# Cross-attention: the values' third round on halves of the array's rows, in two banks; inputs normed a step ahead of their transposes

## The chip, the cores and the metric

The kernel runs on one NeuronCore of a Trainium2 chip. Its engines are TensorE (PE, with the weight loads shown apart as PEld), VectorE (DVE), ScalarE (ACT), GpSimd (POOL) and SyncE (SP); here POOL and SP also issue the DMAs. The metric is the device time of one launch in microseconds (us).

## The reference

The input x is 128 sequences of 32 tokens with 512 channels, the context 128 x 257 x 512. All data is float32. Three blocks follow each other, each on a layer norm of x and added to x: cross-attention, a gated delta-rule layer, and a feed-forward with quantised weights. Only the first is changed:

```python
def _layernorm(x, axis=-1, eps=1e-05):
    m = jnp.mean(x, axis=axis, keepdims=True)
    v = jnp.var(x, axis=axis, keepdims=True)
    return (x - m) / jnp.sqrt(v + eps)
...
q = jnp.einsum('bsd,ed->bse', x, wq)
k_new = jnp.einsum('bsd,ed->bse', x, wk)
v_new = jnp.einsum('bsd,ed->bse', x, wv)
k = jnp.concatenate([k_cache, k_new], axis=1)
v = jnp.concatenate([v_cache, v_new], axis=1)
scores = jnp.einsum('bqd,bkd->bqk', q, k) * scale
attn = jax.nn.softmax(scores, axis=-1)
out = jnp.einsum('bqk,bkd->bqd', attn, v)
return jnp.einsum('bqd,ed->bqe', out, wo)
...
x = x + _L0_xattn_ref(_layernorm(x, axis=-1), mask, ctx_2048, ctx_2048, wq, wk, wv, wo)
```

The context is both the cache of keys and that of values. Each token attends to the 257 rows of its sequence's context and to the 32 tokens of its own sequence: 289 keys.

## The kernel before

Cross-attention takes 128 tokens (four sequences, a "tile") at a time, in 32 steps. Four tiles make a group of 512 tokens; there are eight groups.

At the head of a group, queries and keys of its 512 tokens are projected: 32 float32 matmuls of 128x128x512 (L395), their results copied by ACT and DVE in turn. `hT` holds the normed inputs with channels on partitions; it has been made during the group before.

Each of a group's four steps then does this, and the parts belong to three tiles, so that PE has work while the other engines are busy with the softmax:

- `new_rows` (n): the values of the new tokens are projected (L293), copied to `vn` (DVE, L298), and stored by four POOL DMAs (L300) into `vx`, a tile of 33 partitions: the context's last row (an SP DMA, L289) and 32 new rows, for each of four sequences. A POOL copy (L301) puts the new keys behind the 257 loaded ones in `kall`.
- `turned` (n-1): the 128x289 weights `pr` are transposed on PE in three pieces of 128, 128 and 33 columns (L330) and copied to `prT` by ACT (L332, the first two) and DVE (L333, the third).
- `project` (n-2): the output projection (L360), the residual sum (DVE, L364), a POOL store, and the new statistics (`mean_var`, L81 and L82).
- `values` (n-1): for each sequence j a matmul with 32 columns of weights, so that four run on four column strips of the array. Rounds 0 and 1 take the context's rows, two to a partition (`cx`), 512 columns each; round 2 takes the 33 rows of `vx`. All accumulate in one PSUM bank `av`, which DVE scales into `ao` (L348).
- `weights` (n): the scores (L313), their maximum (L318, L319), the exponential on ACT (L322), the reciprocal of its sum (L323).
- `flipped` (n-1): `ao` is transposed (L97) and copied by ACT (L353).

Two generators are advanced within a step. `quantised_weights` reads the feed-forward's weights in pieces (`raw`), first for a sum of magnitudes (L197), then for three DVE operations (L212 to L214) and a POOL store. `prepared` makes the next group's `hT` in seven slots of which each step takes two, one ahead of the scores and one at its end: loads of three inputs; nothing; load of the fourth; statistics of three; statistics of the fourth and `inverse` (a root on ACT, L246, and a reciprocal on DVE, L247); two inputs normed (`xn`, L241), transposed (L97) and copied by ACT (L242); the other two.

Each engine works through its own queue in order. The order in a queue is not quite that of the source: a scheduler lays it out when the program is built. Root and exponential need different tables in ACT, loaded by an instruction of their own. All PSUM tiles of the stage come from one pool of eight banks; tiles named `xn` have two buffers, `raw` three.

`InOrder` (already there, used in later stages) wraps an engine so that each of its instructions is ordered behind the one before; its instructions are recorded at line 151.

Of the kernel before, what the change touches and what calls it, by code (L numbers as in the profile page):

```python
# [10 lines left out]
FP = mybir.dt.float32  # L11
BF = mybir.dt.bfloat16
AF = mybir.ActivationFunctionType
ALU = mybir.AluOpType
# [4 lines left out]
P = 128  # L19
D = 512  # L20
DC = D // P
NB = 128
T = 32
NT = NB * T
LC = 257
NK = LC + T
# [3 lines left out]
SG = 512  # L30
# [27 lines left out]
class Ctx:  # L58
# [16 lines left out]
        self.eps2 = const.tile([P, 1], FP, name="eps2")  # L75
        nc.vector.memset(self.eps2, LN_EPS * RMS_EPS)

    def mean_var(self, pool, x, mv):

        st = pool.tile([P, 6], FP, name="bn_st")  # L80
        self.nc.vector.bn_stats(st, x)  # L81
        self.nc.vector.bn_aggr(mv, st)  # L82

    def factors(self, mv, rs):

# [133 lines left out]
def cross_attention(g: Ctx, x, ctx_kv, ctxT, wqT, wkT, wvT, woT, x1, stats, scales, ffn_weights):  # L219
# [5 lines left out]
    tc, nc = g.tc, g.nc  # L225
# [3 lines left out]
        ("a_wk", 2), ("a_st", 4), ("a_ps", 8, PSUM),  # L229
    )  # L230
    with stack:
        def load_x(s, i):
            t = xp.tile([P, D], FP, name="xt")
            r = s * SG + i * P
            nc.sync.dma_start(t, x[r : r + P, :])
            return t

        def normed(hT, i, xt, mv, rstd):

            xn = wk.tile([P, D], FP, name="xn")  # L240
            nc.vector.tensor_scalar(xn, xt, mv, rstd, ALU.subtract, ALU.mult)  # L241
            nc.scalar.copy(hT[:, :, i * P : (i + 1) * P], g.transposed(ps, xn, g.ident))  # L242

        def inverse(mv, n):
            rstd = st.tile([P, n], FP, name="rstd")
            nc.scalar.activation(rstd, mv[:, :, 1], AF.Sqrt, bias=g.ln_eps)  # L246
            nc.vector.reciprocal(rstd, rstd)  # L247
            return rstd

        def prepared(s, xt, hT):  # L250


            n = SG // P
            xt.extend(load_x(s, i) for i in range(n - 1))
            yield
            yield
            xt.append(load_x(s, n - 1))
            yield
            mv = st.tile([P, n, 2], FP, name="mv")
            for i in range(n - 1):  # L260
                g.mean_var(st, xt[i], mv[:, i, :])
            yield
            g.mean_var(st, xt[n - 1], mv[:, n - 1, :])
            rstd = inverse(mv, n)
            yield
            for half in range(2):
                for i in range(half * n // 2, (half + 1) * n // 2):
                    normed(hT, i, xt[i], mv[:, i, 0:1], rstd[:, i : i + 1])
                yield

        def load_keys(gi):

# [12 lines left out]

        def new_rows(gi, kall, hT, kT, i):

            vx = cp.tile([T + 1, 4, D], FP, name="vx")
            nc.sync.dma_start(vx[0:1], ctx_kv[gi * 4 : gi * 4 + 4, LC - 1, :].unsqueeze(0))  # L289

            pv = ps.tile([P, D], FP, name="ps")
            for dc in range(DC):
                nc.tensor.matmul(  # L293
                    pv, hT[:, dc, i * P : (i + 1) * P], w["v"][:, dc, :],
                    start=dc == 0, stop=dc == DC - 1,
                )
            vn = wk.tile([P, D], FP, name="vn")
            nc.vector.tensor_copy(vn, pv)  # L298
            for j in range(4):
                nc.gpsimd.dma_start(vx[1 : T + 1, j, :], vn[j * T : (j + 1) * T, :])  # L300
            nc.gpsimd.tensor_copy(  # L301
                kall[:, :, :, LC:NK],
                kT[:, :, i * P : (i + 1) * P].rearrange("p c (b t) -> p c b t", b=4),
            )
            return vx
# [18 lines left out]
            return pr, rs  # L324

        def turned(pr):
            pp = ps.tile([P, 3, P], FP, name="ps")
            for r in range(3):
                m = P if r < 2 else T + 1
                nc.tensor.transpose(pp[0:m, r, :], pr[:, r * P : r * P + m], g.ident)  # L330
            prT = wk.tile([P, 3, P], FP, name="prT")
            nc.scalar.copy(prT[:, 0:2, :], pp[:, 0:2, :])  # L332
            nc.vector.tensor_copy(prT[0 : T + 1, 2, :], pp[0 : T + 1, 2, :])  # L333
            return prT

        def values(cx, vx, prT, rinv):

            av = ps.tile([P, D], FP, name="ps")
            for r in range(3):
                for j in range(4):  # L340
                    js = slice(j * T, (j + 1) * T)
                    if r < 2:
                        lhsT, rhs = prT[:, r, js], cx[:, j, r, :]
                    else:
                        lhsT, rhs = prT[0 : T + 1, 2, js], vx[:, j, :]
                    nc.tensor.matmul(av[js, :], lhsT, rhs, start=r == 0, stop=r == 2)
            ao = wk.tile([P, D], FP, name="ao")
            nc.vector.tensor_scalar_mul(ao, av, rinv)  # L348
            return ao

        def flipped(ao):
# [4 lines left out]
        def project(n, xt, aoT):  # L356

            po = ps.tile([P, D], FP, name="ps")
            for dc in range(DC):
                nc.tensor.matmul(  # L360
                    po, aoT[:, dc, :], w["o"][:, dc, :], start=dc == 0, stop=dc == DC - 1
                )
            xo = wk.tile([P, D], FP, name="xo")
            nc.vector.tensor_add(xo, po, xt)  # L364
            nc.gpsimd.dma_start(x1[n * P : (n + 1) * P, :], xo)
            g.mean_var(st, xo, stats[0][:, n, :])

        xt = [load_x(0, i) for i in range(SG // P)]
        kalls, cxs, quantised = {}, {}, None
# [9 lines left out]
        cxs[1] = load_values(1)  # L379

        hT = sp.tile([P, DC, SG], FP, name="hT")
        for i in range(SG // P):
            mv = st.tile([P, 1, 2], FP, name="mv0")
            g.mean_var(st, xt[i], mv[:, 0, :])
            normed(hT, i, xt[i], mv[:, 0, 0:1], inverse(mv, 1))
        for s in range(NT // SG):
            if s == NT // SG - 1:
                g.factors(*(t[:, 0:EARLY] for t in stats))
# [2 lines left out]
            for wn, dst in ((w["q"], qT), (w["k"], kT)):  # L391
                for ec in range(DC):
                    pp = ps.tile([P, SG], FP, name="ps")
                    for dc in range(DC):
                        nc.tensor.matmul(  # L395
                            pp, wn[:, dc, ec * P : (ec + 1) * P], hT[:, dc, :],
                            start=dc == 0, stop=dc == DC - 1,
# [9 lines left out]
            for i in range(SG // P):  # L407
                n = s * (SG // P) + i
                kall = kalls.pop(n)
                vx = new_rows(n, kall, hT, kT, i)  # L410
                if soft is not None:
                    m, xm, vm, pr, rs = soft
# [468 lines left out]
def delta_out_mlp(  # L881
# [14 lines left out]
    with stack:  # L896
# [105 lines left out]
        def mlp(b):  # L1002
# [14 lines left out]
            for i in range(NTL):  # L1017
                pd = psm.tile([P, D], FP, name="pm")
                for fc in range(FC):
                    nc.tensor.matmul(  # L1020
                        pd, mT[:, fc, i * P : (i + 1) * P], wd[:, fc, :],
                        start=fc == 0, stop=fc == FC - 1,
                    )
                xo = zp.tile([P, D], FP, name="xo", bufs=2)
                mark[:] = [nc.vector.tensor_add(xo, pd, xs[i]).ins]
                n = b * NTL + i
                nc.gpsimd.dma_start(x2[n * P : (n + 1) * P, :], xo)
                g.mean_var(st, xo, mv2[:, n, :])
                z = zp.tile([P, D], FP, name="z")
                nc.vector.tensor_scalar(z, xo, mv2[:, n, 0:1], None, ALU.subtract)  # L1030
                z = butterflies(nc, z, zp.tile([P, D], FP, name="zb"))
                nc.gpsimd.dma_start(z2[n * P : (n + 1) * P, :], z)
                yield 9.5
# [534 lines left out]
```

## Time and profile before

| what | value |
|---|---|
| median of 3 runs | 2940.22 us (2938.33 to 2943.78) |
| the profiled execution | 2938.77 us, span 2937.0 us |
| cross-attention | 0 to some 690 us of the span |
| PE busy over the span | 2823.2 us (96%) |
| DVE, ACT, POOL busy | 1995.4, 1033.0, 682.5 us |
| granted TensorE clock, mean | 0.988 |

The span runs from the first to the last instruction of one execution recorded by the hardware profiler. A row of the order of time gives start, duration, engine, line, operation, out<-in, the tile of the array that a matmul uses (rows*columns), operand shapes and the count of instructions merged; the brackets give the engine's idle time ahead of it and what ended it. A float32 matmul appears as two instructions, a transpose as one. Of matmuls in a row the ends overlap the next starts, so the distance of starts is the time that one takes of PE. Line 151 stands for everything issued through `InOrder` and similar wrappers.

### The profile page before, as it was taken

The page shows a single profiled execution, that of the slowest core. Times are in us where ns is not written, and L with a number is a line of the kernel's source. Part 1 is how long each engine was busy: PE and PEld are TensorE (multiplying, and loading weights), DVE is VectorE, ACT ScalarE, POOL GpSimd, SP SyncE. Part 2 cuts the span into 40 slices and gives each one's busy share as a digit, 9 for nine tenths or more (in the row PEclk, how much of TensorE's full clock was granted, in tenths as well). Part 3 has the DMA queues.
Part 4 walks back from the last instruction along what each step waited for, and adds up shares of the span by engine and source line. Part 5 has one row for each costly group of instructions (what it writes and reads, how often), then busy time and mean ns, then how long its engine had stood idle before and what let it go on. Part 6 is the DMA issues. An engine that isn't in the chain of part 4 may idle for free.

```text
span 2937.0 us, 42773 instructions
## 1 busy us (share of the span) xinstructions
PE 2823.2 (96%) x15895; PEld 1658.6 (56%) x15958; DVE 1995.4 (68%) x3317; ACT 1033.0 (35%) x1766; POOL 682.5 (23%) x974
## 2 busy tenths in 40 slices
PE   8999999997999899999999999999999989999997
PEld 3434343443443344566676767777777756666664
DVE  3353544325599995678787878888722289999996
ACT  1111111213666466521122212112211146776774
POOL 1121212212777677321212111101000000000000
PEclk9999999999999999999999999999999999999999
DMA  9898998874555545841414141313231124434433
GB/s 316 275 306 295 337 315 278 280 243 123 149 165 155 163 141 145 242 140 56 130 54 132 56 130 52 122 57 98 71 108 33 35 74 90 87 81 88 89 71 69
DMA packets 342815, 429.64 MB, mean 146 GB/s; under 512 B 149712, under 2 KB 250192, under 8 KB 340176
## 3 DMA queue, kind: packets, MB, share of 16 engines
q1 hardware_dynamic: 305696, 324.36, 37.0%
q0 software_dynamic: 36912, 102.55, 11.7%
q8 instruction: 127, 2.08, 0.3%
q14 instruction: 80, 0.66, 0.1%
HBM read 288.88 MB, written 94.37 MB: 130 GB/s over the span
## 4 chain that ended last, share of the span: by engine, by line
PE 59%; DVE 10%; issue 2%; DMA 2%; POOL 1%; ACT 1%; SPq 1%; ACTq 0%; DVEq 0%; POOLq 0%
PE ps L151 18%; PE pm L1009 9%; PE pm L1020 9%; PE pm L1012 9%; PE pp L151 5%; PE ps L983 4%; DVE W L503 2%; DVE pr L497 2%; DVE acc L625 2%; PE ps L953 2%; PE pg L151 1%; PE pn L151 1%; DMA xs<-x 1%; POOL kk L541 1%; DVE m L151 1%
## 5 line engine op out<-in xcount | busy, mean ns | idle before, releaser
L1009 PE MATMUL pm<-hT,wg 128*128 128x256 f32 x1408 | 343.1, 386 | 0.2 <-ACT hT L998 0.2
L1012 PE MATMUL pm<-hT,wu 128*128 128x256 f32 x1408 | 336.8, 382 | 1.3 <-DVE wu L1070 1.3
L497 DVE TENSOR_TENSOR pr<-L,W 128x1984 f32<-128x1984 f32 (+30 forms) x248 | 307.3, 1239 | 9.1 <-DMA L<-ld 4.6
L503 DVE TENSOR_TENSOR W<-W,pr 128x1984 f32<-128x1984 f32 (+30 forms) x248 | 309.7, 1249 | 2.8
L1020 PE MATMUL pm<-wd,mT 128*128 128x512 f32 x704 | 307.4, 592 | 0.0
L1009 PEld LDWEIGHTS pm<-hT,wg 128*128 128x128 f32 x1408 | 263.9, 191 | 51.0 <-issue 11.5
L1012 PEld LDWEIGHTS pm<-hT,wu 128*128 128x128 f32 x1408 | 268.7, 191 | 38.7 <-DVE wu L1070 1.6
L1020 PEld LDWEIGHTS pm<-wd,mT 128*128 128x128 f32 x704 | 132.4, 190 | 160.2 <-issue 160.2
L151 PE MATMUL ps<-wq,qT 128*128 128x512 bf16 x930 | 215.5, 379 | 6.2 <-ACT t L151 4.6
L1014 ACT ACTIVATE sg<-pm 128x256 f32<-128x256 f32 x176 | 67.4, 383 | 331.4 <-PE pm L1009 319.7
L1015 DVE TENSOR_TENSOR mT<-pm,sg 128x256 f32<-128x256 f32 x176 | 74.0, 420 | 158.7 <-PE pm L1012 155.0
L151 PEld LDWEIGHTS <-qT 128*128 128x128 bf16 x960 | 94.0, 98 | 105.3 <-issue 5.5
L151 DVE TENSOR_TENSOR mb<-m 128x1024 f32<-128x1024 f32 x128 | 153.2, 1217 | 0.1
L151 DVE TENSOR_TENSOR m<-mb 128x1024 f32<-128x1024 f32 x128 | 150.8, 1219 | 1.2
L1343 POOL DMA_DIRECT2D xo<-x x31 | 26.4, 851 | 526.4 <-ACT xo L151 492.0
L151 ACT ACTIVATE t<-ps,magic,qs 128x512 f32<-128x512 f32 x158 | 115.7, 781 | 39.5 <-DVE qs L151 39.4
L537 POOL DMA_DIRECT2D ld<-kk x128 | 93.6, 731 | 147.6 <-ACT kk L151 120.5
L541 POOL TENSOR_TENSOR kk<-kk,cm 128x256 f32<-128x256 f32 x128 | 126.3, 987 | 2.7
L151 PEld LDWEIGHTS ps<-hd,mT 128*128 128x128 f32 x1024 | 119.1, 192 | 8.9 <-ACT mT L151 4.8
L151 PE MATMUL ps<-hd,mT 128*128 128x128 f32 x1024 | 119.8, 275 | 4.0 <-ACT mT L151 4.0
L151 PE MATMUL ps<-wq,q2T 128*128 128x512 bf16 x481 | 116.2, 384 | 5.4 <-DMA q2T<-q 3.7
L151 PE MATMUL pp<-hT,wk 128*128 128x512 f32 x256 | 120.3, 614 | 0.7 <-ACT hT L151 0.7
(224 smaller groups left out, 4751.2 us busy)
## 6 DMA issues: line engine op xcount, KB each, us to landing
kall<-in_ctxT_dram SPq DMA_DIRECT2D x32, 2056.0 KB
cx<-in_ctx_dram SPq DMA_DIRECT2D x32, 2048.0 KB
x<-xo POOLq DMA_DIRECT2D x64, 256.0 KB, 3.5
ld<-kk POOLq DMA_DIRECT2D x128, 128.0 KB, 2.6
pd<-kk POOLq DMA_DIRECT2D x128, 128.0 KB, 2.6
L<-ld SPq DMA_DIRECT2D x32, 512.0 KB
pe<-pd SPq DMA_DIRECT2D x256, 64.0 KB
kqm<-kq SPq DMA_DIRECT2D x448, 32.0 KB
```

The lines of the kernel that those rows point to most:

```text
L151: got = method(*args, **kw)
L497: nc.vector.tensor_mul(pr[:, 0:n], bc(L[:, s, :, s + 1 : T].rearrange("p h t -> p t h"), HD), w[:, s].unsqueeze(1).to_broadcast([P, n, H4, ...
L503: nc.vector.tensor_sub(w[:, s + 1 :], w[:, s + 1 :], pr[:, 0:n])
L537: nc.gpsimd.dma_start(ld[r].rearrange("(i p) f -> p i f", p=P), kk[:, 0].rearrange("p i h t -> p i (h t)"))
L541: nc.gpsimd.tensor_mul(q, q, cm.unsqueeze(1).to_broadcast([P, 2 * H4, T]))
L625: last = nc.vector.scalar_tensor_tensor(acc[:, :, d:], pp[:, :, : T - d], cw[n][:, ec, TAPS - 1 - d : TAPS - d], acc[:, :, d:], ALU.mult, ...
L983: nc.tensor.matmul(pw, oT[:, i, dc, :], wo[:, dc, :], start=dc == 0, stop=dc == DC - 1)
L1009: nc.tensor.matmul(pg, wg[:, dc, fs], hT[:, dc, :], start=dc == 0, stop=dc == DC - 1)
L1012: nc.tensor.matmul(pu, wu[:, dc, fs], hT[:, dc, :], start=dc == 0, stop=dc == DC - 1)
L1014: nc.scalar.activation(sg, pg, AF.Silu)
L1015: mark[:] = [nc.vector.tensor_mul(mT[:, fc, :], pu, sg).ins]
L1020: nc.tensor.matmul(pd, mT[:, fc, i * P : (i + 1) * P], wd[:, fc, :], start=fc == 0, stop=fc == FC - 1,)
```

## The change

- `vx` gets 128 partitions and half the width: partitions 0 to 32 hold channels 0 to 255 of the 33 rows, partitions 64 to 96 channels 256 to 511. Its context row comes by two DMAs and the new rows by eight.
- `turned` puts the third piece of the transposed weights on both sets of partitions: the transpose as before, and a plain matmul of the same 33 columns with the identity, whose result goes to PSUM partitions 64 to 96. DVE copies both.
- `values` works in two PSUM banks, one for each half of the channels. Rounds 0 and 1 go by halves, 256 columns each; in round 2 each sequence has two matmuls, one on the upper and one on the lower half of the array's rows. DVE scales each bank by itself.
- `prepared` moves the statistics one slot ahead, and the normed inputs stand ahead of their transposes: two are normed in the fifth slot, the sixth transposes them and norms the other two, the seventh transposes those. `inverse` becomes `deviation`, without the reciprocal.
- The first group's inputs go through an `InOrder` DVE: one's statistics, then the reciprocal and norm of the one before.
- `mean_var` takes the engine as an argument. The calls outside this stage do the same as before.

```diff
         def prepared(s, xt, hT):
             n = SG // P
             xt.extend(load_x(s, i) for i in range(n - 1))
             yield
+            mv = st.tile([P, n, 2], FP, name="mv")
             yield
             xt.append(load_x(s, n - 1))
+            for i in range(n - 1):
+                g.mean_var(nc.vector, st, xt[i], mv[:, i, :])
             yield
-            mv = st.tile([P, n, 2], FP, name="mv")
-            for i in range(n - 1):
-                g.mean_var(st, xt[i], mv[:, i, :])
+            g.mean_var(nc.vector, st, xt[n - 1], mv[:, n - 1, :])
+            rstd = deviation(mv, n)
+            nc.vector.reciprocal(rstd, rstd)
             yield
-            g.mean_var(st, xt[n - 1], mv[:, n - 1, :])
-            rstd = inverse(mv, n)
-            yield
-            for half in range(2):
-                for i in range(half * n // 2, (half + 1) * n // 2):
-                    normed(hT, i, xt[i], mv[:, i, 0:1], rstd[:, i : i + 1])
-                yield
+            xn = []
+            for i in range(n + 2):
+                if 2 <= i:
+                    across(hT, i - 2, xn[i - 2])
+                if i < n:
+                    xn.append(normed(nc.vector, xt[i], mv[:, i, 0:1], rstd[:, i : i + 1]))
+                if i % 2:
+                    yield
...
-            vx = cp.tile([T + 1, 4, D], FP, name="vx")
-            nc.sync.dma_start(vx[0:1], ctx_kv[gi * 4 : gi * 4 + 4, LC - 1, :].unsqueeze(0))
+            vx = cp.tile([P, 4, D // 2], FP, name="vx")
+            for h in range(2):
+                nc.sync.dma_start(
+                    vx[h * P // 2 : h * P // 2 + 1],
+                    ctx_kv[gi * 4 : gi * 4 + 4, LC - 1, halves[h]].unsqueeze(0),
+                )
...
             for j in range(4):
-                nc.gpsimd.dma_start(vx[1 : T + 1, j, :], vn[j * T : (j + 1) * T, :])
+                for h in range(2):
+                    r = h * P // 2 + 1
+                    nc.gpsimd.dma_start(vx[r : r + T, j, :], vn[j * T : (j + 1) * T, halves[h]])
...
         def turned(pr):
             pp = ps.tile([P, 3, P], FP, name="ps")
-            for r in range(3):
-                m = P if r < 2 else T + 1
-                nc.tensor.transpose(pp[0:m, r, :], pr[:, r * P : r * P + m], g.ident)
+            for r in range(2):
+                nc.tensor.transpose(pp[:, r, :], pr[:, r * P : (r + 1) * P], g.ident)
             prT = wk.tile([P, 3, P], FP, name="prT")
+            nc.tensor.transpose(pp[last[0], 2, :], pr[:, 2 * P : NK], g.ident)
+            nc.tensor.matmul(pp[last[1], 2, :], pr[:, 2 * P : NK], g.ident, start=True, stop=True)
             nc.scalar.copy(prT[:, 0:2, :], pp[:, 0:2, :])
-            nc.vector.tensor_copy(prT[0 : T + 1, 2, :], pp[0 : T + 1, 2, :])
+            for rows in last:
+                nc.vector.tensor_copy(prT[rows, 2, :], pp[rows, 2, :])
             return prT

         def values(cx, vx, prT, rinv):
-            av = ps.tile([P, D], FP, name="ps")
-            for r in range(3):
-                for j in range(4):
-                    js = slice(j * T, (j + 1) * T)
-                    if r < 2:
-                        lhsT, rhs = prT[:, r, js], cx[:, j, r, :]
-                    else:
-                        lhsT, rhs = prT[0 : T + 1, 2, js], vx[:, j, :]
-                    nc.tensor.matmul(av[js, :], lhsT, rhs, start=r == 0, stop=r == 2)
+            av = [ps.tile([P, D // 2], FP, name="ps") for _ in range(2)]
+            for r in range(2):
+                for h in range(2):
+                    for j in range(4):
+                        js = slice(j * T, (j + 1) * T)
+                        nc.tensor.matmul(
+                            av[h][js, :], prT[:, r, js], cx[:, j, r, halves[h]],
+                            start=r == 0, stop=False,
+                        )
+            for j in range(4):
+                js = slice(j * T, (j + 1) * T)
+                for h in range(2):
+                    nc.tensor.matmul(
+                        av[h][js, :], prT[last[h], 2, js], vx[last[h], j, :], start=False, stop=True
+                    )
             ao = wk.tile([P, D], FP, name="ao")
-            nc.vector.tensor_scalar_mul(ao, av, rinv)
+            for h in range(2):
+                nc.vector.tensor_scalar_mul(ao[:, halves[h]], av[h], rinv)
             return ao
...
-        for i in range(SG // P):
-            mv = st.tile([P, 1, 2], FP, name="mv0")
-            g.mean_var(st, xt[i], mv[:, 0, :])
-            normed(hT, i, xt[i], mv[:, 0, 0:1], inverse(mv, 1))
+        dve = InOrder(tc, nc.vector)
+        got = []
+        for i in range(SG // P + 1):
+            if i < SG // P:
+                mv = st.tile([P, 1, 2], FP, name="mv0")
+                g.mean_var(dve, st, xt[i], mv[:, 0, :])
+                got.append((mv[:, 0, 0:1], deviation(mv, 1)))
+            if i:
+                mv, rstd = got[i - 1]
+                dve.reciprocal(rstd, rstd)
+                across(hT, i - 1, normed(dve, xt[i - 1], mv, rstd))
```

With `halves` = the two slices of 256 channels, `last` = the partitions 0 to 32 and 64 to 96, and `normed` and `across` the two parts of the former `normed` (DVE's norm; PE's transposes and ACT's copy).

## The prediction

> **What bounds the kernel now.** I read the page first, then the busy times by stretch, then the waits, then the order of time inside the first stage (cross-attention, the first 690 us); nothing behind it is changed.
>
> ```profile
> PE 2823.2 (96%) x15895; PEld 1658.6 (56%) x15958; DVE 1995.4 (68%) x3317; ACT 1033.0 (35%) x1766; POOL 682.5 (23%) x974
> ```
>
> The next two rows are stretches of that stage: width, then busy time of PE, PEld, DVE, ACT and POOL, granted clock, DMA share, GB/s. The last row is a wait: total, times, longest.
>
> ```profile
> 165.00:245.00 80.00, 80.00 (x395) 34.26 (x394) 38.77 (x89) 10.45 (x23) 18.30 (x34) 0.99 0.92 304
> 325.00:405.00 80.00, 76.77 (x354) 33.59 (x347) 38.02 (x89) 14.44 (x28) 17.77 (x34) 0.98 0.93 311
> PE ps L97 <- DVE xn L241: 21.9, 5, 8.2
> ```
>
> The stage is bound by TensorE: one stretch has no idle PE at all, the other loses 3.2 us. PE never waits for a load of keys or values, though the DMA engines are over 0.9 busy. So PE work added or removed in a step counts in full, and the only slack to win is PE idle. The wait row shows where: 8.2 us is the start of the kernel, the other 13.7 us are four of the seven changes of group (at 74, 162, 330 and 498 us). The order of time around one of them:
>
> ```profile
> 302.57 0.49 PE L330 MATMUL ps<-ident,pr 128*128 128x128 f32 x3
> 302.89 3.60 PE L360 MATMUL ps<-wo,aoT 128*128 128x512 f32 x8
> 306.42 1.92 PE L346 MATMUL ps<-cx,prT 128*32 128x512 f32 x16
> 308.28 1.06 PE L346 MATMUL ps<-vx,prT 33*32 33x512 f32 x8
> 309.27 2.15 PE L313 MATMUL ps<-kall,qT 128*32 128x289 f32 x32
> 316.94 0.55 PE L330 MATMUL ps<-ident,pr 128*128 128x128 f32 x3 [1.38 <-ACT pr L322]
> 320.95 0.69 DVE L364 TENSOR_TENSOR xo<-ps,xt 128x512 f32<-128x512 f32 x1 [2.69 <-PE ps L360]
> 324.41 0.75 DVE L348 TENSOR_SCALAR ao<-ps,rs 128x512 f32<-128x512 f32 x1
> 325.40 0.69 DVE L81 BATCH_NORM_STATS2 bn_st<-xt 128x6 f32<-128x512 f32 x1
> 325.78 0.66 PE L97 MATMUL ps<-ident,ao 128*128 128x128 f32 x4
> 326.53 0.59 ACT L353 COPY aoT<-ps 128x512 f32<-128x512 f32 x1 [8.58 <-PE ps L97]
> 327.13 1.28 ACT L246 ACT_TABLE_LOAD   x1
> 328.43 0.30 ACT L246 ACTIVATE rstd<-mv,ln_eps 128x4 f32<-128x4 f32 x1
> 328.97 1.00 DVE L241 TENSOR_SCALAR xn<-xt,mv,rstd 128x512 f32<-128x512 f32 x2
> 329.66 1.18 PE L97 MATMUL ps<-ident,xn 128*128 128x128 f32 x8 [3.23 <-DVE xn L241]
> 330.64 5.21 PE L293 MATMUL ps<-wv,hT 128*128 128x512 f32 x8
> ```
>
> What to see: the statistics of the last input end late on DVE, the root on ACT waits behind the copy of aoT and a table load, the normed inputs follow, and PE stands 3.23 us. After it the same eight matmuls take 5.21 us instead of 3.60: the clock is halved for 3.41 us, 1.6 us more.
>
> **Units.** A float32 matmul is two passes. L360's eight passes fill 302.89 to 306.42: 8 x 0.429 + 0.10, so a 512-column pass is 0.429 us and going over to the 32-column tiles costs 0.09 to 0.10. By column a 256-column pass is 0.216 (289 columns: 0.243), a 128-column one 0.109. The first pass in a new mode shows its weight load: 0.025 for 32 columns, 0.105 before a 512-column pass with 128 weights. L330's three transposes take 302.57 to 302.89, 3 x 0.109: the 33-column one switches nothing.
>
> **1. Third round of values on halves.** Before: 308.28 to 309.27, 0.99 = 0.025 + 2 x 0.429 + 0.09 + 0.02 of stagger. After: sixteen passes of 256 columns on eight 64x32 tiles, two rounds: 0.025 + 2 x 0.216 + 0.09 + 0.05 = 0.60. Do eight run together? The nearest row is of this very shape, from the second stage:
>
> ```profile
> 723.35 1.07 PE L151 MATMUL pg<-kqm,kq 64*32 64x256 f32 x24 [1.33 <-DMA kqm<-kq]
> 724.35 0.62 PE L151 MATMUL pn<-sq,hs 128*32 128x512 f32 x1
> ```
>
> 24 passes four at a time would need six rounds, 1.30 us; the next work starts after 1.00, so more than four ran. Gain 0.396 a step, x 32 = 12.7 us. The first two rounds of values go from four rounds of 0.429 to eight of 0.216: +0.01 a step, +0.3 us; their doubled weight loads (0.11) hide under passes of 0.216, as under L313's of 0.243.
>
> **2. Turning the last 33 columns twice.** A plain matmul on a 64-column tile is added: two passes of 128 columns, 0.218. Bounds: nothing more if this tile needs no switch, as the 33-column transpose beside it needs none (0.218 + 0.025, 7.7 us in all); or a switch in and out: 0.093 + 0.025 + 0.218 + 0.093 + 0.105 = 0.534, 17.1 us. Here a rule speaks against the change. The Trainium skill, "TensorEngine Tiling (Array Packing)", sections Key Properties and Restrictions, says that changing the tiling mode drains TensorE, and that column tiling excludes the float32 transpose. By the second sentence the 33-column transpose is not column-tiled at all, so its row says nothing of the new matmul; every real change of tile in this trace (32 columns, 64 rows, both ways) costs 0.09. I take 17.1. By the row alone the final sum would be 8.5 us better (PE then also reaches the waits of part 4 earlier, which gives 0.9 of 9.4 back).
>
> DVE gets one more copy of 33x128 (0.28) and two scalings of 256 columns (some 0.42 each, from 0.28 for 128 and 0.69 for 512) for one of 0.75. Both lie under L313 (2.09 us on PE); without that cover they would cost 0.4 a step.
>
> **3. Queues.** POOL issues 8 stores of 0.50 into vx for 4, +2 us a step; the following x store may wait for the first of the 8 to land (5.6 us after issue), some 2 us. They are read one step (20 us) later, POOL is 23% busy, and the key copy behind them is for scores two steps on: nothing. SP issues one more vx row (0.65), before a load of values that waits for PE anyway: nothing. Without that slack, 2 us a step.
>
> **4. The inputs, a step ahead.** In the built program's order the root's table load now stands right behind the copy of prT, so it hides in ACT's 8.58 us of idle, and the root precedes the copy of aoT. On DVE the changed order at the changes of 162, 330 and 498 us is: xo, five operations on raw weights (1.9), statistics of the last input (0.60), raw (0.34), aggregation (0.14), statistics of xo (0.75), first half of ao, second half, nms, reciprocal, xn. From xo's end, 321.68: statistics done 324.2, first half of ao 325.7, second 326.2, nms 326.5, first xn 327.2, PE at 327.34 for 329.66. PE now waits for ao too, which stands behind more DVE work: L313 ends for it at 325.40, so 1.35 us of idle are left. Does that still halve the clock? In this stage idle of 2.43 (at 485 us) did not, 3.23 always did. So it stays full: 2.32 + 1.65 = 3.97 each, x 3 = 11.9 us. The change at 74 us keeps its idle (same chain: nms, exp, root, about +0.1), the three others have none and get none.
>
> The wait at 316.94 (also 149 and 485 us) hangs on a raw piece that lands at 314.5; two aggregations and a raw operation now stand between it and nms's scaling, +0.30, of which 0.14 would be PE work anyway: +0.5 in all. At the start xn follows its own input: first projections at about 11.4 for 12.56, at half clock, -0.6. End of the stage (ao in halves, one scaling of weights moved into DVE idle): -0.5.
>
> **Sum.** -12.7 + 0.3 + 17.1 - 11.9 + 0.5 - 0.6 - 0.5 = -7.8 us. The profiled execution took 2938.77 us (span 2937.0), 1.45 under the median of 2940.22; its difference is put on the median: **2932.4 us**, -0.27%. About 0.2% (5.9 us) is what a measurement here can tell from no change.
>
> **Rivals.**
> A, no switch for the 64-column tile: -16.3, **2923.9**. For it: the 33-column transpose at 0.109. Against: all other rows.
> B, the halves don't overlap, because they alternate row groups within each column or meet in PSUM: two rounds become four, 12.7 not gained, **2945.1**. For it: vx's eight matmuls each wait on stores of their own. Against: pg's row.
> C, slower: at the three changes the statistics of the last input now stand ahead of ao on DVE. Its load is issued at 309.9 and needed at 323.6 instead of 325.4. A raw piece issued from 299.5 on was awaited until 314.5, so 15 us happen. What is sure is only that it had landed by 325.4: up to 1.8 us late, PE's idle back at 3.1 and the clock halved again from about 1.5 us on. Price 3 x (1.8 + 1.6) = 10.2: +2.4, **2942.6**.
>
> **Chances.** Likeliest 0.55 (own range 2926 to 2939), A 0.25, B 0.08, C 0.12. Two thirds of the likeliest and all of A lie under 2934.3: faster 0.62. The rest of the likeliest, most of C and more than half of B: same 0.28. Slower 0.10 from the tails of B and C and from costs in part 2 above their bound. Range 2921 to 2943: it takes in A with some us below, and C; it leaves out B.
>
> **What would show it.** Right: from the third round's start to L331 0.60 us; from the last transpose of pr to the projection 0.64 instead of 0.11 (0.33 if A); three fewer halved stretches and L97's wait for xn near 1 us at 162, 330 and 498; table load ahead of aoT's copy. Wrong: sixteen passes in four rounds (B); DVE idle ahead of the statistics of xt, ended by a DMA (C); new PE waits for ao in steps that had none; a difference behind 700 us.

## The result and the profile after

The changed kernel took 2938.95 us (median of 12 runs, 2930.34 to 2943.79) beside 2939.73 us for the kernel before (median of 12, 2933.55 to 2947.33): a ratio of 0.9995, 95% interval 0.9984 to 1.0007. The forecast was 2932.4 us, 0.27% faster; what was found is no difference that this measurement can tell. The profiled execution took 2940.0 us (span 2938.2), 1.2 us more than that of the kernel before.

The page's row of busy times after (us, share of the span, instructions):

```profile
PE 2838.9 (97%) x16790; PEld 1684.7 (57%) x16790; DVE 2005.6 (68%) x3381; ACT 1032.7 (35%) x1766; POOL 745.3 (25%) x1102
```

The two stretches of the first stage that were shown of before, and PE's waits in its first 720 us:

```profile
165.00:245.00 80.00, 80.00 (x500) 36.86 (x499) 39.89 (x97) 12.32 (x26) 26.17 (x50) 1.00 0.93 322
325.00:405.00 80.00, 79.30 (x472) 36.32 (x476) 39.64 (x99) 13.23 (x27) 26.29 (x50) 1.00 0.94 323
...
PE ps L97 <- DVE xn L151: 6.6, 3, 6.0
PE ps L97 <- DVE xn L245: 5.6, 4, 3.8
PE ps L348 <- ACT pr L340: 4.0, 3, 1.4
PE ps L97 <- DVE ao L376: 1.7, 4, 0.8
```

The stretch with a change of group in it is now full too (79.30 of 80 us busy, the clock at 1.00 instead of 0.98). The wait for `xn` fell from 21.9 us to 12.2 (the rows of L151, the start, and L245). The same change of group as before, in order of time:

```profile
315.88 0.44 PE L348 MATMUL ps<-ident,pr 128*128 128x128 f32 x2 [1.45 <-ACT pr L340]
316.16 0.27 PE L350 MATMUL ps<-ident,pr 128*33 128x128 f32 x1
316.36 0.41 PE L351 MATMUL ps<-ident,pr 128*33 128x128 f32 x2
316.70 3.70 PE L388 MATMUL ps<-wo,aoT 128*128 128x512 f32 x8
...
317.25 1.28 ACT L253 ACT_TABLE_LOAD   x1
320.33 1.93 PE L364 MATMUL ps<-cx,prT 128*32 128x256 f32 x32
...
322.19 0.66 PE L371 MATMUL ps<-vx,prT 33*32 33x256 f32 x16
...
322.78 2.15 PE L331 MATMUL ps<-kall,qT 128*32 128x289 f32 x32
...
325.08 0.90 PE L97 MATMUL ps<-ident,ao 128*128 128x128 f32 x4
...
326.57 1.11 PE L97 MATMUL ps<-ident,xn 128*128 128x128 f32 x8 [0.59 <-DVE xn L245]
...
327.52 3.60 PE L309 MATMUL ps<-wv,hT 128*128 128x512 f32 x8
```

At this change of group it is, step by step, what was forecast. The third round of values (L371) starts 0.59 us before the scores, 0.99 before the change. From the 33-column transpose (L350) to the projection (L388) there are 0.54 us, and the projection's eight matmuls take 3.70 us instead of 3.60: 0.64 together, the forecast with a change of mode. The idle before `xn` is 0.59 us instead of 3.23, and the eight matmuls behind it take 3.60 us, at full clock. ACT loads the table for the root ahead of the copy of `aoT`. Rivals A (no change of mode) and B (the halves don't overlap) are out by these rows.

In this pair of profiles the first stage does get shorter: its last projection starts at 676.62 us for 683.58 (-6.96), the first transposition of the next stage behind its long wait at 693.77 for 699.54 (-5.77). From there to the last matmul the changed kernel took 2240.3 us and the kernel before 2233.4. So the first question was whether what is behind 700 us takes the gain back.

### The profile page after: what moved, and what is told of

Read it like the earlier page. It is cut to its first block, busy times and chain, and to the rows that moved or that the text cites. A ratio compares the mean times of both kernels' runs of the same rounds, so it can differ in the third digit from the quotient of the medians.

```text
span 2938.2 us, 44870 instructions
## 1 busy us (share of the span) xinstructions
PE 2838.9 (97%) x16790; PEld 1684.7 (57%) x16790; DVE 2005.6 (68%) x3381; ACT 1032.7 (35%) x1766; POOL 745.3 (25%) x1102
## 4 chain that ended last, share of the span: by engine, by line
PE 59%; DVE 9%; DMA 3%; issue 2%; POOL 2%; ACT 1%; SPq 0%; ACTq 0%; DVEq 0%; POOLq 0%
PE ps L151 18%; PE pm L1055 9%; PE pm L1047 9%; PE pm L1044 9%; PE pp L151 5%; PE ps L1018 4%; DVE W L538 2%; DVE pr L532 2%; PE ps L988 2%; DVE acc L660 2%; PE pg L151 1%; POOL kk L576 1%; PE pn L151 1%; DMA kqm<-kq 1%; DMA xs<-x 1%
## 5 line engine op out<-in xcount | busy, mean ns | idle before, releaser
L151 PE MATMUL ps<-wq,qT 128*128 128x512 bf16 x960 | 217.1, 379 | 3.0 <-ACT t L151 3.0
L318 POOL DMA_DIRECT2D vx<-vn x256 | 126.7, 502 | 120.1 <-DVE vn L314 101.8
L151 PEld LDWEIGHTS <-qT 128*128 128x128 bf16 x960 | 94.0, 98 | 103.7 <-issue 3.9
L151 DVE TENSOR_TENSOR mb<-m 128x1024 f32<-128x1024 f32 x128 | 153.2, 1217 | 0.1
L151 DVE TENSOR_TENSOR m<-mb 128x1024 f32<-128x1024 f32 x128 | 150.7, 1219 | 1.2
L151 ACT ACTIVATE t<-ps,magic,qs 128x512 f32<-128x512 f32 x158 | 115.7, 781 | 37.8 <-DVE qs L151 37.8
L151 PEld LDWEIGHTS ps<-hd,mT 128*128 128x128 f32 x1024 | 122.4, 196 | 9.5 <-ACT mT L151 5.3
L151 PE MATMUL ps<-hd,mT 128*128 128x128 f32 x1024 | 123.1, 280 | 4.6 <-ACT mT L151 4.6
L151 PE MATMUL ps<-wq,q2T 128*128 128x512 bf16 x512 | 119.9, 389 | 2.6 <-DMA q2T<-q 2.6
```

Source lines behind the costliest of these rows:

```text
L151: got = method(*args, **kw)
L318: nc.gpsimd.dma_start(vx[r : r + T, j, :], vn[j * T : (j + 1) * T, halves[h]])
```

## The experiments

Ratios and medians are compared within one set of runs on one chip; the kernel before had medians of 2939.7 to 2944.9 us in the different sets.

**The two parts apart.** One kernel has the inputs' part alone, one the values' part alone:

```diff
# e1_inputs_only, against the kernel before
-            for half in range(2):
-                for i in range(half * n // 2, (half + 1) * n // 2):
-                    normed(hT, i, xt[i], mv[:, i, 0:1], rstd[:, i : i + 1])
-                yield
+            xn = []
+            for i in range(n + 2):
+                if 2 <= i:
+                    across(hT, i - 2, xn[i - 2])
...
+        dve = InOrder(tc, nc.vector)
...
# e2_halves_only, against the kernel before
-            vx = cp.tile([T + 1, 4, D], FP, name="vx")
+            vx = cp.tile([P, 4, D // 2], FP, name="vx")
...
+            nc.tensor.matmul(pp[last[1], 2, :], pr[:, 2 * P : NK], g.ident, start=True, stop=True)
...
-            av = ps.tile([P, D], FP, name="ps")
+            av = [ps.tile([P, D // 2], FP, name="ps") for _ in range(2)]
...
```

> Only the inputs' part of the change (normed a step ahead, and the order at the start); the values, the probabilities' transposes and the new rows are those of the kernel before. Stage 1 is read at the first transposition of stage 2 behind its long wait (699.54 us before, 693.77 us changed). Theory 1, the prediction's sum, with what is behind 700 us left to chance: the inputs' terms are -11.9, +0.5 and -0.6, so stage 1 ends at about 687.5 us, no half clock at the three changes of group, and the whole kernel runs about 12 us (0.4%) under the kernel before, give or take the 1.7 us of each stretch of half clock that is there or not there later on. Theory 2, the later stages give back what stage 1 gains, because they start on something that does not move: stage 1 ends at 687.5 us all the same, but the whole is within 0.1% of the kernel before, as the changed kernel is.

> Only the values' part of the change (third round on halves, last 33 columns turned twice, new rows stored in two pieces); the inputs are normed as in the kernel before. Theory 1: -12.7 +0.3 +17.1 = +4.7 us, stage 1 ends at about 704 us with its half clock at the three changes of group as before, and the whole is 0.16% slower than the kernel before. Theory 2, the later stages take up what stage 1 loses or gains: stage 1 ends at 704 us, the whole within 0.1% of the kernel before. If the two parts overlap (each hides some of the other's work), this kernel's and the inputs' kernel's differences of stage 1 do not add up to the -5.8 us of the changed kernel.

Measured, the differences by the ratios: the inputs alone 2936.56 us, ratio 0.9972 (0.9958 to 0.9986), -8.2 us; the values alone 2951.79 us, ratio 1.0021 (1.0010 to 1.0031), +6.2 us, both against 2944.91. Together -2.0 us (-0.07%), near the -0.05% of the whole change. Most of the first stage's gain and loss comes through to the end, so theory 2 (the later stages level it) falls for these two. The first stage ended at 691.79 us with the inputs alone, 4.3 us later than the forecast 687.5, and at 706.15 with the values alone (forecast 704). A step without a wait, between changes of group, is the same to the hundredth in every profile: 12.72 us with the old values, 12.86 with the new ones.

Why did the inputs alone gain 8 and not 12? In its profile the first change of group gained nothing (steps 4 and 5: 33.51 us, before 33.42). In order of time:

```profile
155.22 2.15 PE L324 MATMUL ps<-kall,qT 128*32 128x289 f32 x32
155.37 0.49 DVE L212 TENSOR_SCALAR raw<-raw,inv 128x512 f32<-128x512 f32 x1 [2.19 <-DMA raw<-in_f_w_gateT_dram]
...
158.86 0.66 DVE L81 BATCH_NORM_STATS2 bn_st<-xo 128x6 f32<-128x512 f32 x1
159.44 0.74 DVE L359 TENSOR_SCALAR ao<-ps,rs 128x512 f32<-128x512 f32 x1
...
160.23 1.11 PE L97 MATMUL ps<-ident,ao 128*128 128x128 f32 x4 [2.86 <-DVE ao L359]
...
163.16 5.15 PE L304 MATMUL ps<-wv,hT 128*128 128x512 f32 x8
```

VectorE stands 2.19 us for a piece of the feed-forward's weights; everything behind it in its queue, the statistics and then `ao`, comes late, PE stands 2.86 us for `ao` instead of 3.23 for `xn`, and the clock is halved all the same (5.15 us for eight matmuls). This is rival C's mechanism (a late load ahead of `ao` in VectorE's queue), with another load than the one named. In the changed kernel's first profile PE comes to this place some 2.6 us later, the piece has landed, and the wait isn't there.

**The price of the 64-column tile.** Two kernels turn the last 33 columns without it. The first makes the second copy by one more transposition at full width, of the last 97 columns; the second puts the last 64 columns once more behind `pr` and transposes 97 columns once for both copies:

```diff
# e4_full_width_twice, against the changed kernel
-            nc.tensor.matmul(pp[last[1], 2, :], pr[:, 2 * P : NK], g.ident, start=True, stop=True)
+            w0 = 2 * P - P // 2
+            nc.tensor.transpose(pp[0 : NK - w0, 3, :], pr[:, w0:NK], g.ident)
...
# e3_one_turn, against the changed kernel
+            nc.vector.tensor_copy(pr[:, NK : NK + P // 2], pr[:, NK - P // 2 : NK])
...
-            nc.tensor.transpose(pp[last[0], 2, :], pr[:, 2 * P : NK], g.ident)
-            nc.tensor.matmul(pp[last[1], 2, :], pr[:, 2 * P : NK], g.ident, start=True, stop=True)
+            m = last[1].stop
+            nc.tensor.transpose(pp[0:m, 2, :], pr[:, 2 * P : 2 * P + m], g.ident)
```

> The changed kernel with the second turning of the last 33 columns done as one more full-width transposition, of the last 97 columns, instead of a plain product on a 64-column tile. If the 64-column tile's change of mode is what cost the 0.534 us, a step loses 0.534 and gains the 0.109 us of one pass of 128: -0.425 us in 32 steps, -13.6 us, stage 1 ends at about 680 us and the whole is about 13.6 us under the changed kernel (theory 1) or within 0.1% of it (theory 2). If the cost lay in the plain product and its second pass through PSUM and not in the tile, the transposition would cost about the same and nothing changes.

> The changed kernel with both copies of the last 33 columns out of one transposition: a VectorE copy puts the last 64 columns of the probabilities once more behind them, and 97 columns are transposed at full width, so that the 33 land on rows 0 to 32 and 64 to 96; no tile of 64 columns, one copy out instead of two. Theory 1: the plain product on the 64-column tile and its two changes of mode go, -0.534 us in each of 32 steps, -17.1 us: stage 1 ends at about 676.7 us and the whole is about 17 us under the changed kernel (0.6% under the kernel before or a little more). Theory 2, what stage 1 gains is given back later: stage 1 at 676.7 us, the whole within 0.1% of the changed kernel. Rival on the cost: the copy stands between the exponential and the third transposition and the wait for it shows, 0.1 to 0.2 us a step, then stage 1 ends at 680 to 683 us. Rival on the bound: the loads, at a share of 0.9 of the DMA engines in stage 1, cannot follow, and stage 1 gains less than half of the 17 us, with PE waiting for cx or kall.

Measured: 2928.98 us, ratio 0.9940 (0.9921 to 0.9959), and 2931.01 us, ratio 0.9951 (0.9933 to 0.9969), against 2944.91; the first stage ended at 685.92 and 686.23 us. A plain step takes 12.44 us in the first and 12.33 in the second, for 12.86: -0.42 and -0.53, the forecast -0.425 and -0.534. The order of time of the first:

```profile
557.36 0.38 PE L348 MATMUL ps<-ident,pr 128*128 128x128 f32 x2
557.57 0.27 PE L350 MATMUL ps<-ident,pr 128*33 128x128 f32 x1
557.68 0.27 PE L352 MATMUL ps<-ident,pr 128*97 128x128 f32 x1
557.79 2.74 PE L389 MATMUL ps<-wo,aoT 128*128 128x512 f32 x6
```

Starts 0.11 apart: a 97-column transposition is a pass like any other and switches nothing. So 0.42 of the 0.53 us are the plain product on its tile, its second pass and the changes of mode around it; with 0.11 of that for the second pass, some 0.31 are left for the changes of mode, an estimate from these rows. Both kernels missed their stage's forecast end (680.2 and 676.7), the first by 5.7 and the second by 9.5 us; most of that lies in waits of single steps that were not taken apart. Two waits of the second are of its own making, of 1.0 us at 244 us and this one:

```profile
406.75 0.38 PE L349 MATMUL ps<-ident,pr 128*128 128x128 f32 x2
408.27 0.69 DVE L197 TENSOR_REDUCE sums<-raw 128x1 f32<-128x512 f32 x1 [4.19 <-DMA raw<-in_f_w_downT_dram]
408.88 0.19 DVE L341 COPY pr<-pr 128x64 f32<-128x64 f32 x1
...
409.12 0.35 PE L352 MATMUL ps<-ident,pr 128*97 128x128 f32 x1 [1.99 <-DVE pr L341]
409.31 3.74 PE L388 MATMUL ps<-wo,aoT 128*128 128x512 f32 x5
```

The copy of 0.19 us stood in VectorE's queue behind a sum that waited 4.19 us for a load. Five matmuls then take 3.74 us where they take 2.3: half clock again. ScalarE has just made `pr`; the next kernel has the copy there:

```diff
# e7_one_turn_act, against e3_one_turn
-            nc.vector.tensor_copy(pr[:, NK : NK + P // 2], pr[:, NK - P // 2 : NK])
+            nc.scalar.copy(pr[:, NK : NK + P // 2], pr[:, NK - P // 2 : NK])
```

> The kernel with one transposition of 97 columns, with the copy of the last 64 columns of the probabilities made by ScalarE right behind the exponential instead of by VectorE. If the two waits of 1.0 and 2.0 us for that copy at 244 and 409 us were VectorE's queue (the copy stood behind other work there), they are gone, with the half clock that the second one drew: stage 1 ends at 682 to 683 us instead of 686.2 us, steps stay at 12.33 us, the whole is 3 to 4 us under the kernel with VectorE's copy and about 0.6% under the kernel before. If ScalarE's copy holds up the third transposition, or the copy of the transposed tile behind it, steps grow by 0.1 to 0.3 us and stage 1 ends at 689 us or later.

Its order of time at the same place:

```profile
404.74 0.26 ACT L341 COPY pr<-pr 128x64 f32<-128x64 f32 x1
405.99 0.38 PE L349 MATMUL ps<-ident,pr 128*128 128x128 f32 x2
406.21 0.27 PE L352 MATMUL ps<-ident,pr 128*97 128x128 f32 x1
406.32 1.88 PE L388 MATMUL ps<-wo,aoT 128*128 128x512 f32 x4
```

Both waits are gone, steps stay at 12.33, the stage ends at 681.30 us (forecast 682 to 683). The whole: 2927.88 us against 2941.11, ratio 0.9947 (0.9931 to 0.9962): faster than the kernel before, and in the same set 11.3 us under the changed kernel. Its gain over the kernel with VectorE's copy, 3 to 4 us by forecast and 4.9 at the stage's end, is too small for these intervals to show in the whole.

**Both kernels once more.** Nothing is edited.

> The kernel before, unchanged, profiled once more. From the start of stage 2's transpositions to the last matmul it took 2233.4 us in its first profile, and 2236.8 to 2241.3 us in the profiles of the changed kernel and of the four kernels with parts of it (one of them starts this part later than the kernel before, so it is not the shift). If the first profile of before was a lucky draw of half-clock stretches and waits (theory 1), this one shows 2236 to 2242 us there, with stage 1 again at 699 to 702 us. If the later part really is 6 us quicker in the kernel before (theory 2: the change costs something behind stage 1), it shows 2232 to 2235 us again.

> The changed kernel, unchanged, beside the kernel before on one chip in more rounds. Theory 1: its stage 1 is 5.8 to 7.5 us shorter (the steps of 12.86 us and the changes of 15.04 us come out the same to 0.02 us; only half-clock stretches may differ), and the whole is 0.15 to 0.3% under the kernel before, as the two parts alone gave -0.28% and +0.21%, -0.07% together, at the least -0.05%. Theory 2: the whole is within 0.05% of the kernel before while stage 1 is 5.8 us shorter again, and the later part takes 2239 to 2241 us again beside a shorter one in the kernel before.

The first expectation was wrong twice. The kernel before took 2233.75 us behind its first stage, not 2236 to 2242, and its first stage ended at 695.26 us, not at 699 to 702. The changed kernel took 2233.86 us there this time, not 2239 to 2241, with its first stage ending at 690.99. So the changed kernel need not be longer there: it shows 2240.3 and 2233.9 us. The first stage of the kernel before differs by 4.3 us from profile to profile, and in this pair the changed kernel's was 4.3 us shorter, less than the 5.8 to 7.5 of theory 1. The whole, in 22 runs: 2939.15 against 2941.11 us, ratio 0.9993 (0.9983 to 1.0003). Where the first stage's end moves is seen at the second change of group; the second profile of before:

```profile
328.08 1.06 PE L97 MATMUL ps<-ident,xn 128*128 128x128 f32 x8 [3.23 <-DVE xn L241]
...
328.99 3.60 PE L293 MATMUL ps<-wv,hT 128*128 128x512 f32 x8
```

The same idle of 3.23 us as in the first profile, but the eight matmuls behind it take 3.60 us and not 5.21. The forecast had put half clock behind it in every execution. The Trainium skill, "TensorE: Matmul & The Clock Gate", Part 1 ("What's actually happening"), says that the clock is set by activity in a window of some 3.4 us that runs freely, whatever the kernel does. The traces agree. In each of the 14 profiles of this case all stretches of half clock begin a whole number of 3.413 us apart (in the first profile of before at 74.47, 163.22, 330.47 and 497.73 us: 26, 49 and 49 times), on a grid that lies elsewhere in each execution. The windows of this grid around the idle time, of the first profile of before and then of the second (width, PE's busy time, granted clock, DMA share, GB/s):

```profile
327.06:330.47 3.41, 0.81 (x8) 1.00 1.06 384
330.47:333.88 3.41, 3.41 (x7) 0.50 1.05 412
```

```profile
323.20:326.61 3.41, 1.66 (x24) 1.00 1.08 359
326.61:330.03 3.42, 1.95 (x11) 1.00 1.06 385
330.03:333.44 3.41, 3.41 (x11) 1.00 1.04 410
```

In the first, one window holds 2.60 us of the idle, and the next window has half the clock. In the second the grid cuts the same idle into 1.75 and 1.47 us, and the clock stays full. This border holds between 60 and 655 us of all 14 profiles: each of the 32 windows at full clock with 1.99 us of idle or more was followed by one at half clock, and none of the 2352 with 1.79 or less. Half clock went on for another window where it had itself 0.78 us of idle or more (10 times), and ended at 0.56 or less (32 times). Outside this part, where PE does other work, the border isn't as clean. Of 15 idles of 3.1 to 3.2 us at the three changes (five profiles with the old inputs), 13 were followed by half clock, 2 were cut in halves.

Behind 700 us waits and clock differ too. Of the 7 us more in the changed kernel's first profile, 1.9 come at 1534 us, where PE waits 1.7 us for an ACT copy whose buffer hangs on a store that took 4.41 us instead of 2.51, 1.3 at 1757 us (half clock after an idle of 2.52 us that lies in one window, where before had none after 2.89, cut into 1.69 and 1.20), and 2.6 in the last 40 us. The last stretch of the changed kernel, with all engines' busy times, first and second profile:

```profile
2890.00:2945.00 55.00, 33.65 (x179) 20.74 (x176) 20.41 (x34) 17.74 (x30) 2.61 (x3) 0.84 0.25 53
```

```profile
2890.00:2945.00 55.00, 22.67 (x129) 13.39 (x129) 13.48 (x27) 12.30 (x20) 2.11 (x3) 0.93 0.24 49
```

Same program, the clock at 0.84 and at 0.93. In 33 runs of the kernel before, the 12 with a mean clock of 0.986 or more have a median of 2941.3 us, the 10 with 0.984 or less 2948.8.

**The first stage alone.** The spread of the whole hides a few microseconds, so the stage was also measured by itself; everything behind the cross-attention is left out:

```diff
-        g, x, ctx_kv, ctxT, xwqT, xwkT, xwvT, xwoT, x1, stats, scales,
+        g, x, ctx_kv, ctxT, xwqT, xwkT, xwvT, xwoT, out, stats, scales,
...
-    ffn = HadamardFfn(g, x2, z2, mv2, had, list(zip(fq, scales)), out)
...
-        ffn.run()
```

> Stage 1 alone, of the kernel before: everything behind the cross-attention is left out (the output is what the cross-attention stores), so that its time is measured by itself in many runs and not read from one profile each. The profiles of the whole kernel put the last projection's first matmul at 683.6 and 679.3 us; the end follows some 10 to 15 us later: about 690 to 700 us. The three others of this call are compared with this one by their medians. If the half clock and the waits for the exponential at the three changes of group are there in some executions and not in others, its runs spread over 4 us and more.

> Stage 1 alone, of the changed kernel. The prediction's sum (three windows of half clock saved in every execution): -7.8 us against stage 1 alone of the kernel before, -7.3 without the end. Theory 1 (the half clock at the changes is drawn in some executions only, and the changed kernel draws a longer one at 73 us): -4 to -6 us, as the two pairs of profiles gave -6.9 and -3.8 at the last projection. Theory 2 (the whole gain is not there on average, the first pair was chance): -2 us or less, as the two medians of the whole kernel, -0.8 and -2.0 us.

> Stage 1 alone, with the inputs' part of the change only. The prediction's terms: -12.0 us against stage 1 alone of the kernel before. Theory 1: -8 to -10 us, since part of the half clock is not there in each execution of the kernel before and VectorE's wait for a piece of the other weights can hold the multiply of the attention's rows back at a change (2.9 us at 160 us in its profile). Theory 2: -6 us or less.

> Stage 1 alone, of the kernel with one transposition of 97 columns and ScalarE's copy. Steps of 12.33 us where the changed kernel has 12.86: 0.53 us in each of 32, -17 us against stage 1 alone of the changed kernel, less what a faster PE waits more for the exponential and the loads: -12 to -17. In the whole kernels' profiles the last projection stood at 664.2 us against 676.6 and 675.5 of the changed kernel. If it is under -8, the steps' gain is lost in waits.

> Stage 1 alone, with the values' part of the change only, the fourth corner beside the three measured (698.2 us for the kernel before, 694.1 changed, 688.7 with the inputs' part). The prediction's terms -12.7 +0.3 +17.1 = +4.7 us: 703 us. If the terms of the parts add up, it follows from the other three: 698.2 + (694.1 - 688.7) = 703.6 us. If the values' part costs the more the more idle it meets (its new waits of the projection's scaling show without the inputs' part), 705 us or more; if the idle at the changes of group hides some of it, under 701 us.

| stage 1 alone | median us | lowest to highest | runs | against before, us | forecast, us |
|---|---|---|---|---|---|
| before | 698.25 | 695.64 to 700.76 | 4 | | |
| inputs alone | 688.72 | 687.33 to 694.61 | 4 | -9.5 | -12.0 |
| values alone | 703.76 | 700.66 to 705.06 | 5 | +5.5 | +4.7 |
| the change | 694.09 | 693.04 to 695.45 | 4 | -4.2 | -7.8 |
| one transposition, ScalarE's copy | 680.98 | 678.66 to 683.53 | 5 | -17.3 | |

(The values alone were measured in another set, on another chip.) The parts add: -9.5 + 5.5 = -4.0. The change does shorten its stage, by 4.2 us (the means differ by 4.05, with a standard error of 1.2 from the two spreads), about half of the forecast. In each of the four kernels that were measured both ways the whole gains less, or loses more, than the stage alone, by some 1 to 4 us. The last row is 13.1 us under the change, at the low end of what was expected.

## Where the prediction held and where it failed

The 2938.95 us lie in the stated range of 2921 to 2943, but that range also holds "no difference"; they are 6.5 us above the likeliest value, and "faster" had been given 0.62, "same" 0.28. The mechanism held and the direction of the stage too; the size did not, and 4 us of 2940 lie under the 0.2% that can be told. The forecast put -7.8 us on the whole; the two sets gave -0.8 and -2.0, with intervals of some 3 us to either side, which hold -4.2 but not -7.8. Whether the whole loses 1 to 4 us somewhere behind the stage can't be settled with these intervals. The second pair of profiles shows no such loss, but the five other profiles of whole kernels with parts of the change took 2236.8 to 2243.3 us there, against 2233.4 and 2233.8 of before; the cause stays open.

Where the stage missed is read from the starts of the 32 projections, three profiles of each kernel (two whole, one of the stage alone), means:

| part of stage 1 | before us | after us | difference us | forecast us |
|---|---|---|---|---|
| to the first projection (step 0) | 60.48 | 61.93 | +1.45 | -0.45 |
| step 1 | 19.44 | 20.11 | +0.67 | +0.15 |
| the three changes, two steps each | 3 x 32.94 | 3 x 29.83 | -9.3 | -10.5 |
| the other 24 steps | | | +2.8 | +3.5 |
| last projection starts at | 681.15 | 676.78 | -4.4 | -7.3 |

The forecast column is the prediction's terms laid on these parts: 0.147 for the values in each step, -3.97 and +0.17 for the inputs at each change, -0.6 for the start. The largest miss is step 0 (1.9 us, of which 0.8 to 1.4 are the new stores that part 3 had put at nothing); the steps at the changes make 1.2 and step 1 makes 0.5, and the other steps give 0.7 back.

- **Parts 1 and 2 (values on halves, 33 columns turned twice).** Right: +0.14 a step for +0.147. The Trainium skill's rule that a change of tiling mode drains TensorE ("TensorEngine Tiling (Array Packing)", Key Properties) led to the right size, 0.64 us from the transpose to the projection for 0.11 before, where the row of the 33-column transpose, taken alone, did not. Only the last two steps, which have no scores in them, gain (0.3 and 0.05 us).
- **Part 4, the change of group.** The idle before `xn` fell further than forecast (0.59 us, with 0.15 to 0.19 before `ao`, for 1.35). In the nine changes of each kernel the step with `xn` in it fell from 18.84 to 15.03 us: -3.8, as forecast (-3.97 and +0.15). That it fits so well is partly luck. "3.23 always did" is false (one of these nine drew no half clock), but two others drew a longer stretch, and one had 1.43 us more idle, for `ao`. And the sum counts 0.40 us twice at each change: the 2.32 us are the whole shift of `xn`, with the shorter third round in it (3.23 - 1.35 = 1.88, + 0.40), and part 1 counts that round again, 1.2 us in three changes. What was sized too small is the step ahead of the change, with its wait for the exponential (316.94 us before): put at +0.5 us in all, beside the values' 0.14 it grew by 0.56 at each change, 1.7 in all. Two steps at a change took 29.7 to 34.1 us in the kernel before, 29.2 to 31.2 after.
- **Part 3, "they are read one step (20 us) later ...: nothing".** False in the first step, where the values follow the stores at once. Before the change the third round took 0.99 us there; now 1.43, 2.02 and 1.59 in the three profiles, where 0.60 was forecast. The store queue of the first profile of after and its third round:

```profile
45.22 4.17 POOL L318 DMA_DIRECT2D vx<-vn  x8 [2.42 <-DVE vn L314]
...
52.88 1.50 PE L371 MATMUL ps<-vx,prT 33*32 33x256 f32 x16
53.29 0.61 PEld L371 LDWEIGHTS ps<-vx,prT 33*32 33x32 f32 x6 [0.25 <-DMA vx<-vn]
...
54.31 1.91 PE L331 MATMUL ps<-kall,qT 128*32 128x289 f32 x28
```

Eight stores for four take 4.17 us to issue; the last, issued at 48.88, lands at 53.73, while PE wants it at 52.88. The third round so takes 0.8 to 1.4 us more than forecast, once.

- **The start.** First projections at 11.49 us for 12.56, as forecast (11.4). But the first full clock comes at 14.6, 15.2 and 17.2 us after and 16.4, 16.0 and 11.6 before, as the grid happens to lie. That is 1.0 us later on average, which at half clock costs half a microsecond, the other way.
- **Step 1** has a stretch of half clock of 6.8 us in two of the three profiles of after and of 3.4 in those of before. PE's idle there is about the same (3.8 for 4.0 us), but in those two 1.14 and 1.47 us of it run on into the window at half clock, in the four others 0.10 or less. Where the idle lies on the grid is chance.
- **Rival C** was right in kind, in another kernel: a load that comes late in VectorE's queue ahead of `ao` brings PE's idle and the half clock back (the inputs alone, at 160 us).

"A difference behind 700 us", named as a sign of being wrong, was there in the first pair of profiles and gone in the second: the 7 us of the first pair were no lasting cost of the change. Whether a smaller one remains is open.

## What to carry to other kernels

A saving that is read from the half clock of one profile is a chance, not a sum: here idle time halved the clock where some 2 us of it lay in one window of the 3.41 us grid, and the grid lies elsewhere in each execution. Count the busy passes in full, and the half clock by how often it comes in several profiles. Where one engine is made to wait for another, count a saving ahead of the wait only once. Before adding a pass on a new tile of the array, look for an operand that lands on the wanted rows at full width: here a copied tail of 64 columns made one 97-column transposition do the work of two, and the 0.53 us a step of the extra product and its changes of mode, more than the 0.39 won by the halves, went. Put a small copy that PE waits for on an engine whose queue does not wait for loads, and check the first step by itself when a store is split in more pieces.

## What was not expected of the hardware

- Idle of 1.99 us halved the clock where it lay in one window of the grid (409 us, VectorE's copy), and 3.23 us didn't where the grid cut it in two (328 us in the second profile of before).
- Of the eight small stores of the first step the first three landed 1.7 to 1.9 us after issue, the other five 4.8 to 5.3 (first profile of after).
- A float32 transposition with 33 or 97 columns costs the 0.11 us of any 128-column pass (starts at 557.57, 557.68 and 557.79 us).
